# A selective-scan block on Trainium2: the step sizes by ScalarE's softplus function, in one piece between two table loads

## The chip, the cores and the metric

The kernel runs on one core of a Trainium2 chip. A core has five engines with a queue each: TensorE (PE, matmuls into PSUM), VectorE (DVE, elementwise work and scans), ScalarE (ACT, functions from a table that is loaded in sets), GpSimd (POOL, elementwise work) and SyncE (SP, which issues DMAs). Each engine works through its instructions in the written order and waits on semaphores for the others. The metric is the device time of one execution in microseconds (us). A profiled execution of the kernel also gives the start and end of each instruction.

## The reference

Two layers are applied to eight images of 96 channels and 64x64 pixels. Nearly all of the time goes to the selective scan of the first one. Cut to what matters here:

```python
xs = jnp.stack([s0, s1, s0[..., ::-1], s1[..., ::-1]], axis=1)      # 4 directions, 192 channels, 4096 steps
x_dbl = jnp.einsum('bkdl,kcd->bkcl', xs, x_proj_w)
dts, bs, cs = (x_dbl[:, :, :R], x_dbl[:, :, R:R + N], x_dbl[:, :, R + N:])   # R = 6, N = 16
dts = jnp.einsum('bkrl,kdr->bkdl', dts, dt_projs_w)
delta = jax.nn.softplus(dts + dt_projs_b[None, :, :, None])
A = -jnp.exp(A_logs)
...
def step(hst, inp):
    u_i, dt_i, b_i, c_i = inp
    dA = jnp.exp(dt_i[..., None] * A)
    hst = dA * hst + (dt_i * u_i)[..., None] * b_i[:, :, None, :]
    y = jnp.einsum('bkdn,bkn->bkd', hst, c_i)
    return (hst, y)
```

delta are the step sizes. Around the scan stand a layer norm, a projection, a depthwise 3x3 convolution with silu, a gated output projection, two 3x3 convolutions with a gelu and a channel gate; the second layer is an attention without softmax and a feed-forward in fp8.

## The kernel before

**Units, tiles and slots.** One direction of one image is cut into 8 pieces of 512 steps. Such a piece is a *unit*: 8 images x 4 directions x 8 pieces = 256 units, done one after the other. A unit has 192 channels x 16 states, which lie as 6 tiles of 128 partitions (64 channels, for two halves of the states) x 4 states x 512 steps. The loop over a unit therefore has 24 *slots*, one for each tile and state, 6,144 in all. In each slot ACT makes a decay (`decays`, line 1116: exp of delta times A, into one of four PSUM banks, issued two slots ahead of its use) and DVE runs the recurrence over 512 steps (line 1195).

**Who multiplies with C.** The product of the state with C is either made on DVE, one block of 128x512 after each scan (line 1201; the scan then stays in the PSUM bank of the decay, and is called *banked*), or on POOL for several blocks of a tile at once, in place (`outputs`, line 1002). The table `BANKED` (line 34) says for each tile how many of its four blocks are banked: four in tiles 0, 2 and 4, none in 1 and 3, two or three in tile 5. POOL also makes delta x u x B for each tile (`inputs`, line 994). The last value of each scan is copied by ACT into `carry`, for the next unit (lines 1202 and 1207). TensorE adds the products over the states (`sums`, line 1014).

**The step sizes.** `step_sizes` (line 953) is called with i from 0 to 5. Step 0 is a matmul of the six-row dts with the projection and the bias row, into PSUM bank y01 (128 channels of one unit, "a") or y2 (the other 64 channels of two successive units at once, "b", in odd units only). Steps 1 to 3 are Abs, Exp of the negative and Ln with one added, all on ACT; step 4 on DVE is max(x, 0) plus that; this is softplus. Step 5 on POOL is delta x u. DMAs then spread delta and delta x u over the halves (`spread`, line 982). All of it is made one to two units ahead.

**What sets the order.** `plan` (line 1057) writes by hand which of these steps is issued in which slot. For "a" the six steps stand in slots 6, 8, 9, 10, 11 and 12; for "b" steps 0 to 4 in slots 9, 11, 12, 13 and 15 and step 5 in slot 16, ahead of `outputs` of tile 3. The sums of a unit use the same two PSUM banks from slots 13 and 18 on; they are evacuated in slots 3 and 7 of the next unit (`gather`, line 1038).

**Side streams.** The rest of the computation (the norm, projection and convolution of the next image, and the gated output, convolutions, attention and feed-forward of the last one) is written as generators that are advanced once a slot and put a few instructions into the same queues. They use the activation tables of silu and gelu. Before these they wait in `quiet` (line 269) until the last finished slot is one of those in `CALM`; they then load the table, apply the function and load the table with exp and ln again. At the start of an image the loop waits for streams that have not ended (`drained`, line 713).

Of the kernel before, what the change touches and what calls it, by code (L numbers as in the profile page):

```python
# [9 lines left out]
F32 = mybir.dt.float32  # L10
F16 = mybir.dt.float16
F8 = mybir.dt.float8e5
AF = mybir.ActivationFunctionType
ALU = mybir.AluOpType
# [7 lines left out]
DI, N, R = 192, 16, 6  # L22
T = 512
NC = L // T
G = 4
# [5 lines left out]
SPREAD = 5  # L31
HB = 6

BANKED = ((4, 0, 4, 0, 4, 2), (4, 0, 4, 0, 4, 3))

HOLD = 3
LAND = 11
# [6 lines left out]
def kernel(ctx: ExitStack, tc: tile.TileContext, a, out):  # L44
# [8 lines left out]
    nc = tc.nc  # L53
    P = 128
# [8 lines left out]
    def bank(tag, name):  # L63
        return psum.tile([P, T], F32, tag=tag, name=name, bufs=BANKS[tag])
# [5 lines left out]
    def const(shape, value, name):  # L70
        t = wp.tile(shape, F32, name=name)
        nc.vector.memset(t, value)
        return t

    eps = const([P, 1], 1e-5, "eps")
    one = const([P, 1], 1.0, "one")
# [187 lines left out]

    alone = [False]
    place = [None]
    CALM = (0, 1, 8, 9, 16, 17)

    def quiet():

        while place[0] is not None and place[0] not in CALM:
            yield 1

    def table(name):
        nc.scalar.preload_act_table_set(name)  # L275
# [457 lines left out]
    units, images = [], []  # L733
    for b in range(out.shape[0]):

        s = {"b": b, "done": set(), "live": b + 1 == out.shape[0], "pairs": (1, 0) if b else (0, 1)}
        images.append(s)
        for order, (pair, back) in enumerate((p, k) for p in s["pairs"] for k in range(2)):
            for i in range(NC):
                u = Unit()  # L740
                u.s, u.pair, u.back, u.k = s, pair, back, pair + 2 * back
                u.c, u.start = (NC - 1 - i if back else i), i == 0
                u.order, u.new, u.i = order, (order, i) == (0, 0), len(units)
                u.bc, u.hb, u.delta, u.du, u.p = {}, {}, {}, {}, {}
                u.banked = BANKED[int(b == 0 or u.i % 32 >= NC)]
                units.append(u)

    TILES = [(g, j) for g in range(2) for j in range(3)]
# [14 lines left out]
    dt_w = wp.tile([P, 3, 64], F32, name="dt_w")  # L763
# [159 lines left out]
    sp = scan_pool.enter_context(tc.tile_pool(name="scan", bufs=2))  # L923

    def states(u, what, g):

        t = sp.tile([P, G, T], F32, tag="bc"[what], name="bc"[what])
        r0 = u.back * (XD // 2) + what * N + g * 2 * G
        src = u.s["xd"][u.pair][u.c, r0 : r0 + 2 * G, :].rearrange("(h m) l -> h (m l)", h=2)
        for h in range(2):  # L930
            to = t[64 * h : 64 * h + 64].rearrange("p m l -> p (m l)")
            nc.sync.dma_start(to, src[h].unsqueeze(0).to_broadcast([64, G * T]))
        u.bc[what, g] = t
# [8 lines left out]
    def fetched_u(u):  # L942

        u.ua = sp.tile([P, T], F32, tag="ua", name="ua", bufs=1)
        nc.sync.dma_start(u.ua, u.s["u"][u.pair][0:P, bass.ts(u.c, T)])

    def fetched_pair(u, v):

        u.ub = v.ub = sp.tile([P, T], F32, tag="ub", name="ub", bufs=1)
        for h, w in enumerate((u, v)):  # L950
            nc.sync.dma_start(u.ub[64 * h : 64 * h + 64], w.s["u"][w.pair][P:DI, bass.ts(w.c, T)])

    def step_sizes(us, i):

        u, which = us[0], "ab"[len(us) - 1]
        if i == 0:
            u.ps = bank("y01" if which == "a" else "y2", "dt")
            if which == "a":
                todo = [(u.ps, slice(0, P), u)]
            else:  # L960
                todo = [(u.ps[64 * h : 64 * h + 64], slice(P, DI), w) for h, w in enumerate(us)]
            for ps, d, w in todo:
                nc.tensor.matmul(ps, dt_w.rearrange("r j d -> r (j d)")[32 * w.k : 32 * w.k + R + 1, d], w.dts, start=True, stop=True)  # L963
            u.nat = sp.tile([P, T], F32, tag="nat" + which, name="nat", bufs=1)
            if which == "a":
                u.nata = u.nat
            else:
                for w in us:
                    w.natb = u.nat
        elif i == 1:  # L970
            nc.scalar.activation(u.nat, u.ps, AF.Abs)
        elif i == 2:
            nc.scalar.activation(u.nat, u.nat, AF.Exp, scale=-1.0)
        elif i == 3:
            nc.scalar.activation(u.nat, u.nat, AF.Ln, bias=one)  # L975
        elif i == 4:
            nc.vector.scalar_tensor_tensor(u.nat, u.ps, 0.0, u.nat, ALU.max, ALU.add)  # L977
        else:
            x = u.ua if which == "a" else u.ub
            nc.gpsimd.tensor_tensor(x, u.nat, x, ALU.mult)  # L980

    def spread(u, what, js):

# [10 lines left out]
    def inputs(u, n):  # L994

        g, j = TILES[n]
        hb = u.hb[n] = sp.tile([P, G, T], F32, tag="hb", name="hb", bufs=HB)
        nc.gpsimd.tensor_tensor(hb, u.bc[0, g], u.du[j].unsqueeze(1).to_broadcast([P, G, T]), ALU.mult)  # L998

    def outputs(u, n):  # L1000

        lo = u.banked[n]
        hb = u.hb[n][:, lo:, :]
        nc.gpsimd.tensor_tensor(hb, hb, u.bc[1, TILES[n][0]][:, lo:, :], ALU.mult)  # L1004

# [51 lines left out]
    def plan(u, last, nxt, third, fourth):  # L1057

        at = [[] for _ in range(24)]

        def put(slot, f, *args):
            at[slot].append((f, args))

        if last:
            put(0, outputs, last, 5)
            for m in range(2):
                put(m, sums, last, (3, 4), 2 + m)
            for m in range(2):
                put(3 + m, sums, last, (5,), m)
            put(3, gather, last, 0)  # L1070
            put(7, states, u, 1, 1)
            put(7, gather, last, 1)
        for n in range(6):
            to = (u, n + 2) if n < 4 else (nxt, n - 4)
            if to[0]:
                put(4 * n + 1, inputs, *to)
        if third and u.i % 2:
            put(16, step_sizes, (nxt, third), 5)
        put(8, outputs, u, 1)
        put(16, outputs, u, 3)  # L1080
        for m in range(4):
            put(13 + m, sums, u, (0, 1), m)
            if m < 2:
                put(18 + m, sums, u, (2,), m)
                put(22 + m, sums, u, (3, 4), m)
        put(18, before, u)
        if nxt:
            put(0, spread, nxt, 0, (0, 1))
            put(1, spread, nxt, 1, (0, 1))
            put(10, states, nxt, 0, 0)  # L1090
            put(15, states, nxt, 1, 0)
            put(20, states, nxt, 0, 1)
            if u.i % 2 == 0:
                put(15, spread, nxt, 0, (2,))
                put(16, spread, nxt, 1, (2,))
        if third:
            if third.i < NC:
                put(0, fetched_dt, third)
            put(5, fetched_u, third)
            for i, slot in enumerate((6, 8, 9, 10, 11, 12)):  # L1100
                put(slot, step_sizes, (third,), i)
            if u.i % 2:
                for i, slot in enumerate((9, 11, 12, 13, 15)):
                    put(slot, step_sizes, (nxt, third), i)
                put(17, spread, nxt, 0, (2,))
                put(18, spread, nxt, 1, (2,))
            elif u.i + 3 < len(units):
                put(21, fetched_pair, third, units[u.i + 3])
        if fourth and fourth.i >= NC:
            put(14, fetched_dt, fourth)  # L1110
        return at

    def at_index(i):
        return units[i] if 0 <= i < len(units) else None
# [9 lines left out]
            da[q], u.delta[j], AF.Exp, scale=a_neg[:, u.k, j, g * G + m : g * G + m + 1]  # L1124
        )

    da, kept, side, carry, product = {}, [], [], None, None
    for u in units[:2]:
        fetched_dt(u)
    fetched_u(units[0])  # L1130
    fetched_pair(*units[:2])
    states(units[0], 0, 0)
    for us, js in ((units[:1], (0, 1)), (units[:2], (2,))):
        for i in range(6):
            step_sizes(us, i)
        for what in range(2):
            spread(units[0], what, js)
    for what, g in ((1, 0), (0, 1), (1, 1)):
        states(units[0], what, g)
    fetched_u(units[1])  # L1140
    inputs(units[0], 0)
    inputs(units[0], 1)
    decays(0)
    decays(1)
    for i in range(6):
        step_sizes(units[1:2], i)

    def advance(n):

# [4 lines left out]
    for u in units:  # L1154
        last, nxt, third, fourth = (at_index(u.i + d) for d in (-1, 1, 2, 3))
        if u.new:
            drained(*side)
            b = u.s["b"]
            side = []
# [21 lines left out]
        if u.start:  # L1181
            carry = sp.tile([P, 24], F32, tag="carry", name="carry")
        todo = plan(u, last, nxt, third, fourth)
        for slot in range(24):
            n, m = divmod(slot, G)
            g, j = TILES[n]
# [5 lines left out]
            d = da.pop(q)  # L1192
            banked = m < u.banked[n]
            dd, x = (d[:, ::-1], hb[:, m, ::-1]) if u.back else (d, hb[:, m, :])
            nc.vector.tensor_tensor_scan(dd if banked else x, dd, x, 0.0 if u.start else col, ALU.mult, ALU.add)  # L1195
            if product:
                product()
                product = None
# [4 lines left out]
            elif m == G - 1:  # L1203
                lo = 8 * j + g * G
# [98 lines left out]
```

## Time and profile before

| what | value |
|---|---|
| median of three runs | 10769.01 us (10759.34 to 10769.74) |
| the profiled execution | 10764.72 us, its span 10763.0 us |
| granted clock of TensorE | 0.841 |
| DVE busy | 10158.1 us, 94% of the span |
| POOL busy | 10118.0 us, 94% |
| PE busy | 8423.7 us, 78% |
| ACT busy | 7397.8 us, 69% |
| first scan to last scan | 181.0 to about 10532 us |

In the groups of instructions a row gives the source line, the engine and operation, what is written and read with partitions x elements, the number of instructions, then their busy time and the mean duration of one in nanoseconds, and last how long the engine was idle before them and who ended that idle time. Consecutive instructions of one engine overlap a little, so the distance of two starts is less than a duration. In the list of waits a row gives who waited for whom, the total in us, how often, and the longest. In the order of time a row gives start and duration in us, and in brackets idle time before it. A row of a stretch gives for each engine the busy time and the number of instructions, then clock, DMA share and GB/s.

### The profile page before, as it was taken

To read this page: it belongs to the slowest core of one execution; us is meant where nothing else is said; L and a number is where in the kernel's file an instruction comes from. 1 tells how busy PE (TensorE), PEld (TensorE's weight loads), DVE (VectorE), ACT (ScalarE), POOL (GpSimd) and SP (SyncE) were. 2 spreads that over 40 slices of the span, in tenths; PEclk is the share of its full clock that TensorE was granted. 3 is DMA by queue.
4 is the path that set the end of the run, shared out by engine and by line. 5 is a ranking of instruction groups with operands and counts; after the bars stand their busy time and mean duration, and the time that the engine had idled before them with its cause. 6 is when DMAs were issued, how large, how long until landed. Compare 5 with 4: busy or idle time off the path is not lost. (4 is left out here: it accounts for less than half of the span.)

```text
span 10763.0 us, 97608 instructions
## 1 busy us (share of the span) xinstructions
PE 8423.7 (78%) x23270; PEld 2274.2 (21%) x23270; DVE 10158.1 (94%) x11126; ACT 7397.8 (69%) x15154; POOL 10118.0 (94%) x2782
## 2 busy tenths in 40 slices
PE   7777668886788867888688886888768887677677
PEld 2121112221122211222122221222112221111112
DVE  3999999999999999999999999999999999999993
ACT  4666666777676776777767776677766767666674
POOL 3999999999999999999999999999999999999991
PEclk8888788987889878998789887898778987778788
DMA  6888888998889988898888988889888898888883
GB/s 148 208 205 209 200 209 214 226 226 200 215 216 227 227 193 220 216 231 219 201 218 214 237 212 202 217 220 237 198 211 218 219 235 200 202 203 210 208 214 94
DMA packets 1095381, 2253.29 MB, mean 209 GB/s; under 512 B 435993, under 2 KB 436698, under 8 KB 963731
## 3 DMA queue, kind: packets, MB, share of 16 engines
q1 hardware_dynamic: 1094803, 2247.05, 84.5%
q8 instruction: 184, 3.01, 0.1%
q14 instruction: 394, 3.23, 0.1%
HBM read 1507.14 MB, written 336.69 MB: 171 GB/s over the span
## 5 line engine op out<-in xcount | busy, mean ns | idle before, releaser
L998 POOL TENSOR_TENSOR hb<-b,du 128x2048 f32<-128x2048 f32 x1536 | 6952.6, 4546 | 6.1 <-DMA du<-ua 5.2
L1024 PE MATMUL p<-hb,halves 128*64 128x512 f32 x12288 | 3713.8, 707 | 1053.0 <-POOL hb L1004 562.6
L1123 ACT ACTIVATE da<-delta,w_a_logs 128x512 f32<-128x512 f32 x6144 | 4164.3, 689 | 541.5 <-DVE hb L1195 447.5
L1195 DVE TENSOR_TENSOR_SCAN da<-da,carry,hb 128x512 f32<-128x512 f32 x3311 | 4164.0, 1274 | 90.7 <-ACT carry L1202 37.0
L1004 POOL TENSOR_TENSOR hb<-hb,c 128x2048 f32<-128x2048 f32 (+2 forms) x768 | 2714.3, 3534 | 222.3 <-ACT carry L1207 203.0
L1195 DVE TENSOR_TENSOR_SCAN hb<-da,carry,hb 128x512 f32<-128x512 f32 x2065 | 2547.0, 1265 | 1.8
L1201 DVE TENSOR_TENSOR hb<-da,c 128x512 f32<-128x512 f32 x3784 | 2534.0, 670 | 1.8 <-DMA c<-xd 0.9
L1202 ACT COPY carry<-da 128x1 f32<-128x1 f32 x3784 | 593.8, 157 | 2054.5 <-DVE hb L1201 2045.1
L1024 PEld LDWEIGHTS p<-hb,halves 128*64 128x64 f32 x12288 | 904.8, 157 | 3697.8 <-issue 1876.0
L313 PE MATMUL conv<-f0im,taps 97*128 97x512 f32 (+1 forms) x2088 | 867.7, 655 | 37.2 <-ACT f0pre L369 32.2
L1195 DVE TENSOR_TENSOR_SCAN da<-da,hb 128x512 f32<-128x512 f32 x473 | 566.1, 1214 | 28.0 <-POOL hb L998 26.6
L963 PE MATMUL dt<-dts,dt_w 7*128 7x512 f32 (+1 forms) x1024 | 485.9, 742 | 92.3 <-ACT carry L1207 36.2
L980 POOL TENSOR_TENSOR ua<-nat,ua 128x512 f32<-128x512 f32 x256 | 329.9, 1289 | 170.9 <-DVE nat L977 161.8
L313 PEld LDWEIGHTS conv<-f0im,taps 97*128 97x128 f32 (+1 forms) x2088 | 256.4, 173 | 588.2 <-issue 508.8
L1207 ACT COPY carry<-hb 128x4 f32<-128x4 f32 (+2 forms) x768 | 149.7, 195 | 302.1 <-DVE hb L1195 293.7
L1195 DVE TENSOR_TENSOR_SCAN hb<-da,hb 128x512 f32<-128x512 f32 x295 | 346.8, 1205 | 1.7 <-ACT carry L1202 1.7
L259 PE MATMUL var<-f1e,ones_c 96*96 96x512 f32 x350 | 225.6, 731 | 121.8 <-ACT f1e L256 68.5
L253 PE MATMUL ctr<-f1e,cen_c 96*96 96x512 f32 x402 | 218.1, 649 | 86.1 <-ACT f1e L592 34.2
L977 DVE SCALAR_TENSOR_TENSOR nat<-dt,nat 128x512 f32<-128x512 f32 x384 | 258.0, 672 | 17.9 <-ACT nat L975 12.7
L975 ACT ACTIVATE nat<-nat,one 128x512 f32<-128x512 f32 x384 | 271.8, 708 | 0.1
L497 PE MATMUL cab<-f1im,cab_w 97*32 97x512 f32 x1044 | 256.0, 603 | 12.5 <-DMA f1im<-xld 7.1
L275 ACT ACT_TABLE_LOAD x193 | 247.6, 1283 | 4.1 <-PEq L1292 0.8
(430 smaller groups left out, 7586.0 us busy)
## 6 DMA issues: line engine op xcount, KB each, us to landing
b<-xd SPq DMA_DIRECT2D x1024, 512.0 KB
c<-xd SPq DMA_DIRECT2D x1024, 512.0 KB
delta<-nat SPq DMA_DIRECT2D x1536, 128.0 KB
du<-ua SPq DMA_DIRECT2D x1024, 128.0 KB
y<-yt SPq DMA_DIRECT2D x512, 256.0 KB
u<-y SPq DMA_DIRECT2D x384, 256.0 KB
ua<-u SPq DMA_DIRECT2D x256, 256.0 KB
du<-ub SPq DMA_DIRECT2D x512, 128.0 KB
```

The source lines that it names most:

```text
L313: nc.tensor.matmul(ps, taps[:, t, lo : lo + n], im[:, r0 + dy : r0 + dy + 8, dx : dx + HW], start=t == 0, stop=t == 8,)
L963: nc.tensor.matmul(ps, dt_w.rearrange("r j d -> r (j d)")[32 * w.k : 32 * w.k + R + 1, d], w.dts, start=True, stop=True)
L975: nc.scalar.activation(u.nat, u.nat, AF.Ln, bias=one)
L977: nc.vector.scalar_tensor_tensor(u.nat, u.ps, 0.0, u.nat, ALU.max, ALU.add)
L980: nc.gpsimd.tensor_tensor(x, u.nat, x, ALU.mult)
L998: nc.gpsimd.tensor_tensor(hb, u.bc[0, g], u.du[j].unsqueeze(1).to_broadcast([P, G, T]), ALU.mult)
L1004: nc.gpsimd.tensor_tensor(hb, hb, u.bc[1, TILES[n][0]][:, lo:, :], ALU.mult)
L1024: nc.tensor.matmul(ps, halves, u.hb[n][:, i, :], start=TILES[n][0] == 0 and m == 0, stop=False, skip_group_check=True)
L1123: nc.scalar.activation(da[q], u.delta[j], AF.Exp, scale=a_neg[:, u.k, j, g * G + m : g * G + m + 1])
L1195: nc.vector.tensor_tensor_scan(dd if banked else x, dd, x, 0.0 if u.start else col, ALU.mult, ALU.add)
L1201: nc.vector.tensor_tensor(x, d, c, ALU.mult)
L1202: kept.append(lambda: nc.scalar.copy(col, d[:, at : at + 1]))
```

## The change

Steps 1 to 4 of the step sizes become one Softplus activation, which reads the PSUM bank once. The steps are split: `step_sums` issues the matmul ("a" in slot 6, "b" in slot 8), `step_sizes` in slot 9 loads the softplus table, applies it to "a" and, in odd units, to "b", and loads the table with exp and ln again; `scaled_input` is the product on POOL, at the old places. At the start of the program the same is done for the first units. `CALM` loses slots 8 and 9. `BANKED` gets new entries: tile 5 has four banked blocks in every fourth of those units that had three, and three in all others; where all four are banked, `outputs` of that tile is left out.

```diff
-BANKED = ((4, 0, 4, 0, 4, 2), (4, 0, 4, 0, 4, 3))
+BANKED = ((4, 0, 4, 0, 4, 3), (4, 0, 4, 0, 4, 4))
...
-    CALM = (0, 1, 8, 9, 16, 17)
+    CALM = (0, 1, 16, 17)
...
-                u.banked = BANKED[int(b == 0 or u.i % 32 >= NC)]
+                u.banked = BANKED[int((b == 0 or u.i % 32 >= NC) and u.i % 4 == 0)]
...
-        elif i == 1:
-            nc.scalar.activation(u.nat, u.ps, AF.Abs)
-        elif i == 2:
-            nc.scalar.activation(u.nat, u.nat, AF.Exp, scale=-1.0)
-        elif i == 3:
-            nc.scalar.activation(u.nat, u.nat, AF.Ln, bias=one)
-        elif i == 4:
-            nc.vector.scalar_tensor_tensor(u.nat, u.ps, 0.0, u.nat, ALU.max, ALU.add)
...
+    def step_sums(us):
+
+        which = "ab"[len(us) - 1]
+        ps = bank("y01" if which == "a" else "y2", "dt")
+        if which == "a":
+            todo = [(ps, slice(0, P), us[0])]
+        else:
+            todo = [(ps[64 * h : 64 * h + 64], slice(P, DI), w) for h, w in enumerate(us)]
+        for to, d, w in todo:
+            nc.tensor.matmul(to, dt_w.rearrange("r j d -> r (j d)")[32 * w.k : 32 * w.k + R + 1, d], w.dts, start=True, stop=True)
+        dt_sums.append((us, ps))
+
+    def step_sizes():
+
+        table("softplus")
+        for us, ps in dt_sums:
+            which = "ab"[len(us) - 1]
+            nat = sp.tile([P, T], F32, tag="nat" + which, name="nat", bufs=1)
+            nc.scalar.activation(nat, ps, AF.Softplus)
+            for w in us:
+                if which == "a":
+                    w.nata = nat
+                else:
+                    w.natb = nat
+        table("natural_log_exp_and_others")
+        dt_sums.clear()
...
     def outputs(u, n):
 
         lo = u.banked[n]
+        if lo == G:
+            return
...
         if third and u.i % 2:
-            put(16, step_sizes, (nxt, third), 5)
+            put(16, scaled_input, (nxt, third))
...
-            for i, slot in enumerate((6, 8, 9, 10, 11, 12)):
-                put(slot, step_sizes, (third,), i)
+            put(6, step_sums, (third,))
             if u.i % 2:
-                for i, slot in enumerate((9, 11, 12, 13, 15)):
-                    put(slot, step_sizes, (nxt, third), i)
+                put(8, step_sums, (nxt, third))
+            put(9, step_sizes)
+            put(12, scaled_input, (third,))
+            if u.i % 2:
                 put(17, spread, nxt, 0, (2,))
                 put(18, spread, nxt, 1, (2,))
```

More of the change, by code (lines that the diff above doesn't have):

```diff
@@ L951, in fetched_pair @@
             nc.sync.dma_start(u.ub[64 * h : 64 * h + 64], w.s["u"][w.pair][P:DI, bass.ts(w.c, T)])
[L953 to L969, printed above, removed]
-        elif i == 1:
-            nc.scalar.activation(u.nat, u.ps, AF.Abs)
-        elif i == 2:
-            nc.scalar.activation(u.nat, u.nat, AF.Exp, scale=-1.0)
-        elif i == 3:
-            nc.scalar.activation(u.nat, u.nat, AF.Ln, bias=one)
-        elif i == 4:
-            nc.vector.scalar_tensor_tensor(u.nat, u.ps, 0.0, u.nat, ALU.max, ALU.add)
-        else:
-            x = u.ua if which == "a" else u.ub
-            nc.gpsimd.tensor_tensor(x, u.nat, x, ALU.mult)
@@ L982, in spread, with scaled_input @@
+    def scaled_input(us):
+        nat, x = (us[0].nata, us[0].ua) if len(us) == 1 else (us[0].natb, us[0].ub)
+        nc.gpsimd.tensor_tensor(x, nat, x, ALU.mult)
     def spread(u, what, js):
@@ L1125, in decays @@
         )
-    da, kept, side, carry, product = {}, [], [], None, None
+    da, kept, side, carry, product, dt_sums = {}, [], [], None, None, []
     for u in units[:2]:
@@ L1132 @@
     states(units[0], 0, 0)
+    for us in (units[:1], units[:2]):
+        step_sums(us)
+    step_sizes()
     for us, js in ((units[:1], (0, 1)), (units[:2], (2,))):
-        for i in range(6):
-            step_sizes(us, i)
+        scaled_input(us)
         for what in range(2):
@@ L1140 @@
     fetched_u(units[1])
+    step_sums(units[1:2])
+    step_sizes()
     inputs(units[0], 0)
@@ L1144 @@
     decays(1)
-    for i in range(6):
-        step_sizes(units[1:2], i)
+    scaled_input(units[1:2])
     def advance(n):
```

## The prediction

> **What bounds the kernel now.** I read the page first (busy shares, then the costliest groups), then the busy time by stretches of 500 us, then the list of what VectorE (DVE) waited for, and last the order of instructions in time on ScalarE (ACT) and DVE around the place that is edited.
>
> From the page: the busy line and the groups that the change touches.
>
> ```profile
> PE 8423.7 (78%) x23270; PEld 2274.2 (21%) x23270; DVE 10158.1 (94%) x11126; ACT 7397.8 (69%) x15154; POOL 10118.0 (94%) x2782
> ...
> L1201 DVE TENSOR_TENSOR hb<-da,c 128x512 f32<-128x512 f32 x3784 | 2534.0, 670 | 1.8 <-DMA c<-xd 0.9
> ...
> L977 DVE SCALAR_TENSOR_TENSOR nat<-dt,nat 128x512 f32<-128x512 f32 x384 | 258.0, 672 | 17.9 <-ACT nat L975 12.7
> L975 ACT ACTIVATE nat<-nat,one 128x512 f32<-128x512 f32 x384 | 271.8, 708 | 0.1
> ...
> L275 ACT ACT_TABLE_LOAD x193 | 247.6, 1283 | 4.1 <-PEq L1292 0.8
> ```
>
> Two engines, DVE and GpSimd (POOL), are both busy 94% of the whole span. The stretches say that the missing 6% lies mostly in the start and the end, and that which of the two is full changes on the way (columns: PE, weight loads, DVE, ACT, POOL, clock, DMA share, GB/s):
>
> ```profile
> 500.00:1000.00 500.00, 369.20 (x1008) 105.59 (x1010) 487.78 (x521) 328.71 (x675) 499.97 (x136) 0.82 0.85 207
> ...
> 4500.00:5000.00 500.00, 444.26 (x1338) 124.00 (x1338) 492.18 (x540) 358.00 (x730) 486.58 (x132) 0.92 0.91 228
> ```
>
> During image 0 POOL has no idle time at all; later both have about 2 to 4%. Of what DVE waits for in its scans, POOL is 63 us and ACT's carry copies 37 (its decays, not shown, 17):
>
> ```profile
> DVE da L1195 <- POOL hb L998: 62.9, 67, 6.9
> ...
> DVE da L1195 <- ACT carry L1202: 37.0, 19, 3.2
> ```
>
> So for images 1 to 7 the time is DVE's own work and its short waits for ACT; POOL follows closely behind. What decides this change is whether ACT can stop making decays for some microseconds in the middle of each unit without DVE noticing. The order in time shows how much lead ACT has there. An even unit, first ACT, then DVE:
>
> ```profile
> 4553.21 0.69 ACT L1123 ACTIVATE da<-delta,w_a_logs 128x512 f32<-128x512 f32 x1
> 4553.83 0.58 ACT L971 ACTIVATE nat<-dt 128x512 f32<-128x512 f32 x1
> 4554.31 0.68 ACT L1123 ACTIVATE da<-delta,w_a_logs 128x512 f32<-128x512 f32 x1
> ```
>
> ```profile
> 4557.96 0.67 DVE L1201 TENSOR_TENSOR hb<-da,c 128x512 f32<-128x512 f32 x1
> 4558.55 0.67 DVE L977 SCALAR_TENSOR_TENSOR nat<-dt,nat 128x512 f32<-128x512 f32 x1
> 4559.14 1.27 DVE L1195 TENSOR_TENSOR_SCAN hb<-da,carry,hb 128x512 f32<-128x512 f32 x1
> ```
>
> The two decays are those of the scans of slots 10 and 11 (a decay is issued two slots ahead); that of slot 12 follows at 4555.62. The scan at 4559.14 is that of slot 12.
>
> The kernel already has such interruptions: silu and gelu change the table twice each. In image 0 one fell just here (ACT, then the DVE scan that it delayed):
>
> ```profile
> 792.73 1.28 ACT L275 ACT_TABLE_LOAD   x1
> 794.03 1.48 ACT L321 ACTIVATE f0pre<-f0pre 128x1536 f32<-128x1536 f32 x1
> 795.53 1.28 ACT L275 ACT_TABLE_LOAD   x1
> 796.82 0.69 ACT L1123 ACTIVATE da<-delta,w_a_logs 128x512 f32<-128x512 f32 x1
> ```
>
> ```profile
> 797.55 1.29 DVE L1195 TENSOR_TENSOR_SCAN da<-da,carry,hb 128x512 f32<-128x512 f32 x1 [1.81 <-ACT da L1123]
> ```
>
> **The change, part by part.** The sum is made against the profiled execution, 10764.7 us (span 10763.0), 4 us under the median of the three runs, 10769.0, and within their spread.
>
> *DVE loses the max-and-add of line 977.* 384 instructions; back to back each takes 0.59 us (4558.55 to 4559.14; the 672 ns of the row overlap the next one). 384 x 0.59 = 227 us less, all on DVE. The 17.9 us for which DVE stood idle before them go too.
>
> *DVE gains products with C.* By the two tables of banked counts, 200 units had 15 and 56 had 14: 3784, as the row says. Afterwards 50 units (every fourth of those 200) have 16 and 206 have 15: 3890. That is 106 more, 0.41 per unit. At 0.59 us (4557.96 to 4558.55) this is 63 us more. Net work of DVE: -164 us.
>
> *POOL loses the same 106 blocks.* Kept apart by shape, its last product of a unit took 1291 ns for one block (200 times) and 2362 ns for two (56 times): 258 + 132 = 390 us. Afterwards 206 x 1.291 = 266 us: -124 us. Where DVE sets the time this is worth nothing directly. In image 0 it is the limit: 8 of its 32 units lose one block, 10 us, while DVE's saving there is 32 x (1.5 x 0.59 - 0.25 x 0.59) = 24 us; so 14 us of DVE's saving do not show.
>
> *ACT loses three passes of 384* (222.9 + 237.5 + 271.8 = 732 us) and gets 384 softplus passes and two table loads for each of 256 blocks. No row has a softplus; the nearest are Abs on the same operands (0.580 us) and Ln with a bias pointer (0.708 us). I take 0.58, since operands and shape are those of Abs. The loads: 512 x 1.29 (795.53 to 796.82) = 660 us. ACT in sum: -732 + 223 + 660 = +151 us of 10,763, at 69% busy; as a total it does not matter. What matters is that it is one piece: 1.29 + 0.58 + 1.29 = 3.16 us in even units, 3.66 us in odd ones (the second pass overlaps by 0.08), between the decays of the scans of slots 11 and 12. Behind it in ACT's queue stand a carry copy, the decay of slot 12 and what the side streams ask of ACT; DVE waits for that decay at the scan of slot 12.
>
> The even unit above: without Abs the decay of slot 11 starts at 4553.83 and ends at 4554.51; the piece ends at 4557.67, the carry copy (0.18) at 4557.85, the decay of slot 12 (0.69) at 4558.54. Without line 977 the scan could start at 4558.55. So the piece just fits, with no margin. An odd unit is 0.5 us over unless ACT had run ahead. Every side operation of ACT in those slots is then paid by DVE in full. ACT's remaining work, beyond decays (4164), carry copies (594 + 150) and the three passes (732), is about 1,600 us over 6,144 slots, 0.26 us a slot, and it comes in lumps of 0.6 to 1.5 us. Ends: nothing per unit (every piece fits as in the unit shown), and the silu row less what is shorter: 1.81 - (4.09 - 3.16) = 0.88 us in even, 1.38 us in odd units, 1.13 on average, 289 us. The unit shown is the nearer row, as it has the kernel's own order at that slot and the silu comes a slot earlier, where ACT has just come out of four slots without products; I take 0.35 us a unit (about half of it the odd units' 0.5, the rest lumps): +90 us.
>
> *The matmuls of the step sizes move.* That for 128 rows stays in slot 6 and is read in slot 9 instead of 8. That for the pair moves from slot 9 to 8 and is read in slot 9 instead of 11. TensorE runs behind where two convolutions overlap: ACT waited 35.9 us in 33 of 384 cases for these matmuls, at most 4.7. Now such a wait would stand inside the piece. Ends: 0 and 128 x 0.6 = 77 us; I take 15, as the table load and the first pass (1.87 us) come before the pair is read.
>
> *What costs nothing.* The products nat x u on POOL stay at their places in its queue (slots 12 and 16) and find nat earlier than before. PSUM banks y01 and y2 come free in slot 9 rather than 11 and 15, before the sums of slots 13 and 18 need them. DMA issues are the same and in the same queue places, but for side-stream stores behind a later silu. Silu and gelu may no longer start in slots 8 and 9. Counted through the code, four silus of image 0 did; all streams of the other images end in the same slot as before, so no image ends later for it. If one did, DVE and POOL would stand still for the steps left over, a slot each (10,350 us / 6,144 = 1.7 us).
>
> Sum: -164 - 18 + 14 + 90 + 15 = -63 us: 10,702 for a run like the profiled one; I say 10,700.
>
> One rule speaks against the change. The Trainium skill, "ScalarE: Activation LUTs", section "What ACT_TABLE_LOAD costs", gives 1283 ns for the load, as the row here, and 1380 ns more for a drain at each switch. In the trace above the next activation starts 1.30 and 1.29 us after a load's start, so no such drain stands there. By the page's figure each piece would be 2.76 us longer, and the estimate would be up to 256 x 2.76 = 700 us slower.
>
> **The rivals.**
> 1. *The piece isn't hidden (slower).* Place: the scan of slot 12, waiting for the decay. For it: the silu row, 1.81 us; odd units have no margin; after the piece ACT starts slots 12 to 15, where DVE needs only 1.2 us a slot, without a lead. Against it: the even unit's arithmetic, and no further DVE wait within 5 us behind the silu. Price 289 us: -164 - 18 + 289 + 15 = +122, 10,890. It decides from 0.65 us a unit on.
> 2. *All hidden, and POOL's relief counts too (much faster).* No stall: -164 - 18 = -182; and DVE's 62.9 us of waits for POOL go: 10,520 to 10,580. Against it: odd units; and POOL still has (10,118 - 124) / 256 = 39.0 us of work a unit, as much as DVE.
> 3. *POOL becomes the bound everywhere, or stalls eat the gain:* within 21 us of before. POOL's work falls by only 124 us, and its waits (203.0 us for carry copies on ACT) may grow with ACT's delays.
>
> **How the numbers follow.** A measurement of this kernel tells 0.2% (21 us) from no change. Forecast, a gain of 21 to 130 us: 0.54 (own range 10,640 to 10,745). Rival 2 and its neighbourhood, below 10,640: 0.10. Rival 3: 0.11. Rival 1, from +21 us to its full price: 0.25. So faster 0.64, same 0.11, slower 0.25. For 8 in 10 the range leaves out about 0.07 below 10,610 and 0.12 above 10,860.
>
> **What the profile after would show.** Right: the max-and-add row gone, 3890 products, 705 table loads of 1283 ns, softplus near 0.58 us; DVE's waits for ACT at the scan of slot 12 near 90 us in all, more in odd units; DVE busy about 9,995 us; POOL about 9,995. Wrong: waits of DVE for ACT above 165 us in sum; a drain behind the loads; ACT waiting for the pair's matmul in most odd units; or POOL idle no longer while DVE's idle time grows.

## The result, and the profile after

The changed kernel takes 10800.9 us (median of 8 runs, 10794.0 to 10805.1) against 10768.2 us before: 1.0032 times, 95% interval 1.0021 to 1.0043. It is slower by 33 us, where 68 us less were forecast.

The work went as forecast, the waiting did not. The page of the changed kernel, busy line and the groups touched (columns as before):

```profile
PE 8566.6 (79%) x23270; PEld 2293.4 (21%) x23270; DVE 10015.9 (93%) x10848; ACT 7636.8 (71%) x14954; POOL 9994.5 (93%) x2732
...
L1210 DVE TENSOR_TENSOR hb<-da,c 128x512 f32<-128x512 f32 x3890 | 2599.3, 668 | 1.8 <-DMA c<-xd 0.8
...
L275 ACT ACT_TABLE_LOAD x705 | 904.5, 1283 | 13.7 <-PEq L1301 0.8
```

VectorE (DVE) has 142 us less to do (10158.1 to 10015.9) and GpSimd (POOL) 124 us less. Both are less busy than before, in a longer span: neither is kept full. In the list of what DVE waited for (who waited for whom, us in total, times, longest), changed kernel:

```profile
DVE da L1204 <- POOL hb L1001: 96.1, 80, 17.7
...
DVE f1e L465 <- PE attn L463: 57.5, 32, 5.2
DVE da L1204 <- ACT carry L1211: 55.9, 31, 3.2
...
DVE hb L1204 <- ACT carry L1211: 51.3, 66, 3.3
...
DVE da L1204 <- ACT da L1129: 28.7, 43, 1.9
...
DVE hb L1204 <- ACT da L1129: 8.9, 17, 1.8
```

The list of the kernel before had these for the same waits:

```profile
DVE f1e L465 <- PE attn L463: 23.8, 18, 5.2
...
DVE hb L1195 <- ACT carry L1202: 1.7, 6, 0.3
```

Adding the rows of both lists by who waited for whom gives the account of the change:

| DVE | before, us | after, us | difference |
|---|---|---|---|
| busy | 10158.1 | 10015.9 | -142 |
| max-and-add (line 977) waits for ACT | 17.2 | none | -17 |
| scans wait for ACT (carry copies and decays) | 55.5 | 144.8 | +89 |
| other operations wait for ACT | 310.3 | 340.5 | +30 |
| other operations wait for TensorE (PE) | 109.9 | 143.1 | +33 |
| scans wait for POOL | 62.9 | 102.1 | +39 |

The differences add up to +32 us; the span grew by 38.7 us (10763.0 to 10801.7).

The scans stand in the trace in their written order, 24 to a unit, so that each wait can also be counted by its slot (that of the last scan that DVE had started). The lists don't show this split; it changes the reading of three rows:

| DVE's waits | before, us | after, us |
|---|---|---|
| scans for ACT, slot 12 | 0 | 52 |
| scans for ACT, slots 19 and 20 | 44 | 81 |
| other operations for ACT, slots 9 to 11 | 42 | 98 |
| other operations for ACT, everywhere else | 268 | 242 |

Of the +39 for POOL, 15 stand ahead of the very first scan. It waits 17.7 us instead of 2.5, but starts earlier than before (at 179.0 us, then 181.0), because DVE's waits for ACT ahead of it (line 977 among them) are shorter by about as much. These two cancel. Half of the other 24 us are in image 0.

Three places show how the waits look. First, an even unit in which a side stream kept ScalarE (ACT) back. ACT, changed kernel:

```profile
4316.36 0.59 ACT L255 ACTIVATE f1e<-ctr 96x512 f32<-96x512 f32 x1 [1.67 <-PE ctr L253]
...
4318.04 1.28 ACT L275 ACT_TABLE_LOAD   x1
4319.33 0.60 ACT L971 ACTIVATE nat<-dt 128x512 f32<-128x512 f32 x1
4319.95 1.28 ACT L275 ACT_TABLE_LOAD   x1
4321.24 0.16 ACT L1211 COPY carry<-da 128x1 f32<-128x1 f32 x1
4321.44 0.69 ACT L1129 ACTIVATE da<-delta,w_a_logs 128x512 f32<-128x512 f32 x1
```

and DVE's scan of slot 12, which needs the decay at 4321.44:

```profile
4322.23 1.28 DVE L1204 TENSOR_TENSOR_SCAN hb<-da,carry,hb 128x512 f32<-128x512 f32 x1 [2.29 <-ACT carry L1211]
```

The piece itself is as forecast: the loads end 1.29 us after they start, softplus takes 0.60 us. But ACT came to it late, after 1.67 us of waiting for TensorE, and the scan pays for that. (The list names the carry copy; it is the decay right behind it that the scan needs.)

Second, a side operation. In slot 9 the gated output's stream issues a Square on ACT, behind the piece, and a product on DVE that waits for it. ACT, then DVE:

```profile
4405.75 1.28 ACT L275 ACT_TABLE_LOAD   x1
4407.04 0.59 ACT L449 ACTIVATE f1pre<-dy 64x512 f32<-64x512 f32 x1
```

```profile
4407.67 0.69 DVE L450 TENSOR_TENSOR f1pre<-dy,f1pre 64x512 f32<-64x512 f32 x1 [3.10 <-ACT f1pre L449]
4408.39 1.23 DVE L1204 TENSOR_TENSOR_SCAN da<-da,hb 128x512 f32<-128x512 f32 x1
```

The decay of the scan at 4408.39 had been made from 4401.94 to 4402.63; the scan stands behind the side operation in DVE's queue, which waited 3.10 us.

Third, TensorE. The pair's matmul, one slot earlier, now stands ahead of a side stream's two attn matmuls (PE, changed kernel):

```profile
3052.38 1.50 PE L962 MATMUL dt<-dts,dt_w 7*64 7x512 f32 x4
3053.81 2.02 PE L462 MATMUL attn<-f1x,wy_a 128*96 128x512 f32 x2
3055.76 2.02 PE L463 MATMUL attn<-f1pre,wy_b 64*96 64x512 f32 x2
```

```profile
3057.82 0.69 DVE L465 TENSOR_TENSOR f1e<-attn,f1e 96x512 f32<-96x512 f32 x1 [4.20 <-PE attn L463]
```

Before, the attn matmuls stood ahead of the pair's (PE) and the same product of DVE waited 0.38 us:

```profile
3049.28 1.10 PE L463 MATMUL attn<-f1pre,wy_b 64*96 64x512 f32 x2
...
3051.36 1.07 PE L963 MATMUL dt<-dts,dt_w 7*64 7x512 f32 x4
```

```profile
3050.41 0.69 DVE L465 TENSOR_TENSOR f1e<-attn,f1e 96x512 f32<-96x512 f32 x1 [0.38 <-PE attn L463]
```

The order is not the whole of it. The attn matmuls also take twice as long here as there, 2.02 against 1.02 us, and the granted clock of TensorE differs (third number from the end): 0.50 in the stretch of the changed kernel, 1.00 in that of the kernel before.

```profile
3053.80:3057.80 4.00, 4.00 (x7) 0.88 (x5) 0.00 (x0) 3.59 (x7) 4.00 (x2) 0.50 0.44 102
```

```profile
3047.36:3051.36 4.00, 4.00 (x9) 1.16 (x9) 3.62 (x6) 3.85 (x9) 4.00 (x1) 1.00 1.02 215
```

This place, slot 10 of unit 7, comes back in images 1 to 7. There the product waits 27.2 us in all in the changed kernel, each time at clock 0.50, and 4.1 us before. In three of the runs below with the same order of matmuls (two more loads, softplus alone, Exp and Ln) the clock was 1.00 at most of these places, and a wait there was 1.3 to 2.3 us. By these, seven waits of the order alone would be 9 to 16 us (an estimate), so that it explains about half of the increase at most; why the clock was 0.50 just here, no run shows.

### The profile page after: what moved, and what is told of

Same layout as the page of the kernel before. It is cut to its first block, busy times and chain, and to the rows that moved or that the text cites. A ratio compares the mean times of both kernels' runs of the same rounds, so it can differ in the third digit from the quotient of the medians.

```text
span 10801.7 us, 96773 instructions
## 1 busy us (share of the span) xinstructions
PE 8566.6 (79%) x23270; PEld 2293.4 (21%) x23270; DVE 10015.9 (93%) x10848; ACT 7636.8 (71%) x14954; POOL 9994.5 (93%) x2732
## 5 line engine op out<-in xcount | busy, mean ns | idle before, releaser
L1029 PE MATMUL p<-hb,halves 128*64 128x512 f32 x12288 | 3786.8, 706 | 791.0 <-POOL hb L1009 630.7
L1204 DVE TENSOR_TENSOR_SCAN da<-da,carry,hb 128x512 f32<-128x512 f32 x3385 | 4258.5, 1273 | 129.5 <-ACT carry L1211 55.9
L1009 POOL TENSOR_TENSOR hb<-hb,c 128x2048 f32<-128x2048 f32 (+1 forms) x718 | 2587.7, 3604 | 395.5 <-ACT carry L1216 373.6
L1210 DVE TENSOR_TENSOR hb<-da,c 128x512 f32<-128x512 f32 x3890 | 2599.3, 668 | 1.8 <-DMA c<-xd 0.8
L1204 DVE TENSOR_TENSOR_SCAN hb<-da,carry,hb 128x512 f32<-128x512 f32 x1991 | 2451.4, 1264 | 65.2 <-ACT carry L1211 49.2
L1204 DVE TENSOR_TENSOR_SCAN da<-da,hb 128x512 f32<-128x512 f32 x505 | 605.3, 1214 | 56.4 <-POOL hb L1001 54.0
L1216 ACT COPY carry<-hb 128x4 f32<-128x4 f32 (+1 forms) x718 | 140.1, 195 | 323.5 <-DVE hb L1204 318.5
L1204 DVE TENSOR_TENSOR_SCAN hb<-da,hb 128x512 f32<-128x512 f32 x263 | 308.1, 1205 | 3.4 <-ACT carry L1211 2.1
L657 PE MATMUL ff<-f1x,q_w 96*128 96x512 fp8e5 x174 | 83.0, 477 | 254.2 <-DVE f1x L653 150.9
L534 PE MATMUL cab<-f1m,cab_w 96*96 96x512 f32 x348 | 213.8, 735 | 54.4 <-ACT f1e L543 25.8
```

What stands on the lines that cost most here:

```text
L1029: nc.tensor.matmul(ps, halves, u.hb[n][:, i, :], start=TILES[n][0] == 0 and m == 0, stop=False, skip_group_check=True)
L1210: nc.vector.tensor_tensor(x, d, c, ALU.mult)
```

## The experiments

Theory P: the lost time is DVE waiting in, and behind, the piece in which ACT makes no decays. Theory Q: the piece is hidden, and the loss is the 106 products that went from POOL to DVE. Each run was compared with runs of the kernel before on the same chip; intervals are 95%.

**The piece without its table loads.**

```diff
-        table("softplus")
         for us, ps in dt_sums:
...
-            nc.scalar.activation(nat, ps, AF.Softplus)
+            nc.scalar.activation(nat, ps, AF.Abs)
...
-        table("natural_log_exp_and_others")
         dt_sums.clear()
```

> The changed kernel without the two table loads of each piece, and with Abs in place of Softplus (the step sizes are then another function; same operands, same duration). Theory P, the piece: the 180 us of idle time that VectorE gained are the piece's 3.2 to 3.7 us without decays, so without the loads (2.6 us of it) most of them go, and the saving of VectorE shows: 10,570 to 10,640 us. Theory Q, the rebalance: the time is lost because VectorE got 106 products (63 us) for which GpSimd's relief is of no use, and the piece is hidden; then this run stays within 30 us of the changed kernel, 10,770 to 10,800.

10679.6 us, 0.9922 of before (0.9907 to 0.9937), 121 us less than the changed kernel. Q falls: the moved products are all still there. P has the direction, but the run misses its numbers by 40 us on the slow side. DVE's list says why:

```profile
DVE da L1202 <- POOL hb L999: 129.2, 108, 17.1
```

The scans' waits for ACT are back to 71 us in all (144.8 in the changed kernel), at slot 12 to 1 us (52), and other operations in slots 9 to 11 wait 58 us for ACT (98). But the waits for POOL are twice those of before (62.9); 17 us of them stand ahead of the first scan. With DVE freed, POOL is the next limit, a term that the forecast had put at 14 us for image 0 and nothing elsewhere.

**The piece with two more loads.**

```diff
         table("softplus")
+        table("natural_log_exp_and_others")
+        table("softplus")
         for us, ps in dt_sums:
```

> The changed kernel with four table loads in front of and behind the softplus of each piece instead of two: 2.58 us more in each of 256 pieces, 660 us of ScalarE time. P: the lead of the decays is used up already, so 70 to 100% is paid: 11,260 to 11,460 us. Q: the piece still lies under VectorE's work in most units: less than 100 us more, 10,800 to 10,900.

11264.3 us, 1.0466 (1.0450 to 1.0481): 463 us more than the changed kernel for 660 us of loads, 70%, just at the edge of P's range; Q falls again. By slots it stands at the scan of slot 12, whose waits for ACT grow from 52 to 514 us. Other operations in slots 9 to 11 wait 215 us for ACT instead of 98, and the waits for POOL fall by 74 us. The largest row of DVE's list:

```profile
DVE hb L1206 <- ACT carry L1213: 469.1, 187, 5.8
```

The two runs together give the price of a pause on ACT at this place: the first 2.58 us a unit cost 121 us (18% of 660), the next 2.58 us cost 463 us (70%). So ACT's lead at this place is used up by about one piece. (The 18% may be a little low, as the run without loads gives some of its gain back in waits for POOL.)

The mean granted clock went with the time in these three kernels: 0.840 without loads, 0.832 in the changed kernel, 0.824 with two more loads. It doesn't show as the cause in the last one: DVE waits less for TensorE there (118 us) than in the changed kernel (143).

The Trainium skill, "ScalarE: Activation LUTs", section "What ACT_TABLE_LOAD costs", adds a drain of 1380 ns to each switch. No run here shows it: the three loads in a row of this kernel took 3.86 us together, and ACT's next instruction started 0.01 us later.

```profile
4713.50 3.86 ACT L275 ACT_TABLE_LOAD   x3
4717.37 1.08 ACT L973 ACTIVATE nat<-dt 128x512 f32<-128x512 f32 x2
```

**Softplus alone.** The changed kernel with the `BANKED` table, its use and the `CALM` slots of before.

> Softplus and its pieces as in the changed kernel, but the old shares of products with C and the old places for silu and gelu. P: VectorE has 63 us less to do and GpSimd 124 us more, which then limits: 10,790 to 10,830, no better than the changed kernel. Q: without the moved products the gain of the softplus shows: 10,690 to 10,740.

10772.1 us, 1.0008 (0.9999 to 1.0017): no change that can be told. Neither theory's number is met. DVE's busy time is 9952.7 us, 205 less than before, and none of it shows: scans wait 159 us for ACT (+103) and 124 us for POOL (+61), other operations 363 us for ACT (+53, without those of line 977).

**The shares alone.** The kernel before with the new `BANKED`.

> The kernel before with only the new shares of products with C (106 more on VectorE, 63 us; 124 us less on GpSimd). P: by itself about half of VectorE's 63 us, as GpSimd's waits shrink too: 10,780 to 10,820. Q: all of it, and the same loss as the whole change: 10,800 to 10,830.

10792.4 us, 1.0027 (1.0017 to 1.0037), 28 us slower; DVE is busy 10220.3 us, 62 more. So P's range holds. The two halves add up: +7 and +28 against +33 for both, which leaves nothing for `CALM` if the parts don't act on each other. The forecast had credited softplus alone with about 126 us less (-63 for all, less the 63 of the products).

**Exp and Ln without loads.** Softplus as Ln(1 + Exp(x)): like softplus it needs no max-and-add, and both functions are in the table that the decays use. It holds for x under 88 only.

```diff
-        table("softplus")
         for us, ps in dt_sums:
...
-            nc.scalar.activation(nat, ps, AF.Softplus)
+            nc.scalar.activation(nat, ps, AF.Exp)
...
+            exps.append(nat)
-        table("natural_log_exp_and_others")
         dt_sums.clear()
 
+    def step_logs():
+
+        for nat in exps:
+            nc.scalar.activation(nat, nat, AF.Ln, bias=one)
+        exps.clear()
...
             put(9, step_sizes)
+            put(10, step_logs)
```

> The changed kernel with Ln(1 + Exp(x)) in place of Softplus, Exp in slot 9 and Ln in slot 10, no table loads; it holds for x under 88, where Exp has not overflowed. VectorE's saving is kept, ScalarE has 384 passes more than without loads, in two pieces of about 0.6 to 1.3 us. If the loads are the cost (121 us between the two kernels measured), 10,680 to 10,720 us. If the cost is that the passes stand together at slots 9 and 10 at all, 10,740 us or more.

10689.4 us, 0.9928 (0.9913 to 0.9942). The loads are the cost; that the passes stand together is not. The same with the old shares:

> The same with the old shares of products with C. Theory that GpSimd is the next limit: 106 blocks (124 us) are back on it, VectorE loses 63 us, and the time is that of the new shares or up to 40 us more. Theory that VectorE stays the limit once the loads are gone: 28 us less than with the new shares, as the shares alone measured.

10680.5 us, 0.9923 (0.9907 to 0.9940). This can't be told from the new shares: 9 us lie between the medians, and one theory had asked for none or more, the other for 28 less. Of the 63 us that DVE saves, 53 are given back in waits, for POOL above all (147 us at the scans against 108), as the first theory has it.

**The piece behind the side streams.** The piece is issued at the end of slot 9 rather than ahead of the streams' instructions.

```diff
-            put(9, step_sizes)
...
             place[0] = slot
             advance(slot)
+            if slot == 9 and dt_sums:
+                step_sizes()
```

> The changed kernel with the piece issued behind the side streams' instructions of slot 9 instead of ahead of them. If a part of the loss is that VectorE's side operations wait in its queue for ScalarE results behind the piece, that part (about 60 us of idle time) falls: 10,740 to 10,780 us. If it only moves to the scan of slot 12, which then waits for the side operations and the piece, nothing is gained: 10,790 to 10,830.

10761.6 us, 0.9993 (0.9984 to 1.0003), 39 us less than the changed kernel. The waits of other operations for ACT fall from 340.5 to 309.2 us, those for TensorE stay (138); the scans' waits for ACT fall from 144.8 to 135.8. So some 40 us of the loss were the order of the piece and the side streams in one slot. By slots it isn't one wait that goes: other operations in slots 9 to 11 wait 24 us less for ACT (98 to 74) and the scans of slots 19 and 20 29 us less (81 to 52), while the scan of slot 12 waits 18 us more (52 to 70). Why slots 19 and 20 are touched stays open. With the old shares as well:

> Softplus piece behind the side streams of slot 9, with the old shares of products with C. If the two corrections add up (39 us for the order, 29 us for the shares): 10,725 to 10,745 us. If GpSimd, with 106 blocks back, is then the limit: 10,755 us or more.

10736.7 us, 0.9974 (0.9963 to 0.9985). The two corrections add up, and with them the softplus function is a small gain. The same two, with Exp and Ln:

> Exp and Ln without table loads and with the old shares, both issued behind the side streams of their slots (9 and 10). If the order costs by what stands in front of the side streams' results, two passes of 0.6 to 1.3 us cost little there: 10,665 to 10,685 us, the same as with them ahead. If the order matters as such, 20 to 40 us less.

10664.9 us, 0.9904 (0.9888 to 0.9921), the fastest kernel of the study. It is 16 us below its fellow with the passes ahead of the streams (10680.5), at the lower edge of the first expectation by the median, and the intervals of the two overlap: whether the order matters here stays open.

**The pair's matmul back in slot 9.**

```diff
             if u.i % 2:
-                put(8, step_sums, (nxt, third))
+                put(9, step_sums, (nxt, third))
             put(9, step_sizes)
```

> The changed kernel with the pair's matmul back in slot 9 on TensorE, directly ahead of the piece, instead of slot 8. If its move ahead of the side streams' attn matmuls makes VectorE wait for these (about 34 us more in the list of waits than before), that wait goes: 10,765 to 10,785 us. If the softplus of the pair now waits for its matmul within the piece, the scan of slot 12 waits longer in odd units and the time rises: 10,805 to 10,850 us.

10800.3 us, 1.0031 (1.0020 to 1.0043): the same as the changed kernel, between the two expectations, because both happen. The product that waited 4.20 us for the attn matmuls waits 0.39 us:

```profile
3057.53 0.69 DVE L465 TENSOR_TENSOR f1e<-attn,f1e 96x512 f32<-96x512 f32 x1 [0.39 <-PE attn L463]
```

and the softplus waits for its matmul within the piece, 65.3 us in 51 cases (9.4 us in the changed kernel), which the scans behind it pay:

```profile
DVE hb L1204 <- ACT carry L1211: 89.0, 83, 3.3
```

against 51.3 us in the changed kernel. By slots it is the scan of slot 12 in odd units, where the pair is made: 71 us against 32, with 20 us in even units in both kernels. DVE's waits for TensorE fall by 25 us (143 to 118). The time is the same, but the comparison is not clean: at the place shown the granted clock was 1.00 in this run and 0.50 in the changed kernel, so that not all of the 25 us are the order's.

## Why the prediction was wrong

The time is inside the stated range, but the sign is wrong. Point by point:

- *DVE's work, -164 us:* 142 were found, 3890 products as counted. The products cost what was forecast (62 us in the run with the shares alone, 63 forecast); the max-and-add was worth 205 us (softplus alone) and not 227. The 22 us that are missing fit the overlap of neighbouring instructions (0.06 to 0.08 us each), which is lost where DVE waits between them; that is argued, not tried. *POOL's work, -124 us:* right to the microsecond. *The waits before line 977, -18:* they went, but 13 us of them stood ahead of the first scan and came back there as a wait for POOL.
- *The piece at the scan of slot 12, +90 us:* the scans' waits for ACT grew by 89 us, but that the totals agree is luck. At slot 12 they are 52 us, in 62 of the 256 units, more in odd ones (32) than in even ones (20), as forecast. The other 37 us stand at the scans of slots 19 and 20, for which the forecast had nothing. At one of them (unit 18 of image 1, 2.66 us instead of 0.88) a silu between its two table loads stands ahead of the decay on ACT; what links these waits to the piece stays open. Lead, order and softplus's 0.60 us were read rightly from the timeline; the price of slot 12 was too high by 38 us.
- *The pair's matmul, +15 us:* the mechanism was wrong. ACT waits less for these matmuls than before (9.4 us against 35.9). Instead DVE's side operations wait for TensorE, +33 us. Of these, 23 stand behind the attn matmuls of unit 7, partly for the order of the matmuls and partly for a granted clock of 0.50 there. In the last run the matmul's old place cost as much, in another wait.
- *"Every side operation of ACT in those slots is then paid by DVE in full"* is the step that failed. It was priced at the scan only. DVE's queue also holds side operations in slots 9 to 11 that wait for ACT's results behind the piece, and these hold up scans whose decays are long ready: +56 us in these slots (42 to 98; the account shows +30, as such waits fall by 26 us elsewhere). They follow the length of the piece, 58 us without the loads and 215 with two more. The term was missing from the sum. ACT's work beyond the rows named there was also put too low, at about 1,600 us: its busy time less these rows leaves 1,758, 0.29 us a slot.
- *ACT's total, +151 us:* its busy time rose by 239 us (7397.8 to 7636.8). As the text said, the total did not matter; where it stands did.
- *POOL, +14 us:* measured +39 in the scans' waits for POOL, of which 15 stand ahead of the first scan and cost nothing. Of the other 24 half is in image 0, near the forecast, and half in images 1 to 7. The text's own remark, that POOL has as much work a unit as DVE, was used against rival 2 and not in the sum.

Lost overlap 22, side operations 30, TensorE 33 less the 15 forecast, and 25 more for POOL are 95 us; the forecast of -68 us missed the measured +33 by 101. These are differences of the lists, in which some waits cancel, and not prices that each stand alone. Rival 1 had the right sign, but slot 12 reached 52 us of its 289: the loss came from several places. The waits of DVE's scans for ACT ended at 145 us, below the 165 us given as the mark of failure, because that mark counted one kind of wait.

## What to carry to other kernels

Where two or three engines are full and tied by queues, an edit that takes work from one and puts a pause on another must be priced at every consumer in the queue behind the pause, side work included, and not only at the one that the pause was fitted to. A pause on an engine with a lead is cheap until the lead is used up: here 18% of the first 2.6 us was paid and 70% of the next. Before a function with a table of its own is used, see whether the functions of the table that is already loaded give it: Exp and Ln without loads kept most of the saving that softplus lost, and with the side streams' instructions ahead and the old shares it is 0.96% faster than the kernel before.

## What was not expected of the hardware

A table load took 1.283 us in every case (705 in the changed kernel, 1217 with two more a piece), and in the rows shown ACT's next instruction began within 0.02 us of its end, between activations and after three loads in a row. Taking 205 us of work from an engine that was busy 94% of the time changed the total by less than the measurement tells in one order of instructions (softplus alone), and 29 to 101 us were gained from about the same saving in others (the softplus piece, and Exp and Ln, both behind the side streams with the old shares).
